# Graph layer and attention layer on one core: projections from block products in float32 to three float32r passes, with another order of layer 0

## The chip, the cores and the metric

The kernel runs on one core of a Trainium2 chip. The metric is the device time of one execution in microseconds (us), the median of several. The profile is of one more execution, taken by the hardware profiler; its durations belong to that execution.

## The reference, cut to what matters

```python
x, adj: (64, 256, 512) float32, (256, 256) int32 (0 or 1)
# layer 0
mi, mj = x @ Wi.T, x @ Wj.T                       # 512 -> 512 each
out = deg[None, :, None] * (mi + b) + einsum('ij,bjo->bio', a, mj)
x = layernorm(x + out)
# layer 1: 8 heads of 64
q, k, v = (x @ W.T + bias for q, k, v)            # 512 -> 512 each
p = softmax(where(adj == 0, -inf, q k^T / 8))
out = (p v, heads side by side) @ Wo.T + bo
x = layernorm(x + out)
```

64 batches of 256 nodes and 512 channels pass through both layers. All is float32.

## The kernel before, in words

A host-side launch (L1085 on) transposes the weights. The device program has a fast path, `unshifted_path` (L237), and a `general_path` (L58) that a flag calls when the fast path's numbers would not hold; it does not run here.

**Tiles.** 128 partitions, so a batch has two row blocks (NT = 2) and four channel blocks (NC = 4). Two batches form a pair (NB = 2), 32 pairs. The main loop (`for g in range(NG - 1)`, L973) runs 31 times: in turn g it makes the attention of pair g, layer 0 of pair g+1, the output projection of pair g, and the query, key and value projections of pair g+1. The opening ahead of it makes layer 0 and the projections of the first pair, and prepares weights; the tail makes the last pair's attention. `in_order` (L281) makes an instruction keep its place in the program's order; all of TensorE's have it, and so the order of the calls in the loop is the order of TensorE's work. Waits come from a framework that sets a semaphore wait wherever an instruction needs a result or a free buffer. Each engine runs its own queue in order.

**Projections.** Each of the four projections of a pair, a 512 x 512 by 512 x 512 product, is done by seven block products of 256 x 256 x 256 (`pair_steps`, L656; Strassen's scheme in Winograd's form), in float32. `left_steps` (L476) makes four sums of blocks of the left side (tiles hS and oS) on VectorE. The weights' sums are made once in the opening (`make_factors`, L411) and kept in DRAM; `bring` (L437) fetches one factor of 256 KB into a ring of nine, in the order of use, by SP's queue. The `use` functions (L680 to L755) evict each product, with adds on VectorE, copies on ScalarE and adds on GpSimd; several products share an intermediate `u`.

**Layer 0.** `l0_steps` (L502) makes one batch's layer 0 from seven products too, but with weights that lie in SBUF (`w0`): step1 to step7, two float32 matmuls of 512 columns each. They use PSUM banks x, y, z, w; x, y and z take two products each, and the second accumulates onto the first after the first has been read: y by step4 then step6, z by step5 then step7. Step5 copies z to `mj`, step6 makes u3 and adds it to `mj` on GpSimd, step7 makes the other half of `mj`. `split` cuts `mj` into a head and a remainder in float32r (`hi` by ScalarE, `lo` by GpSimd), and `neighbours` (L569) multiplies both by the graph's matrix, eight float32r matmuls of 512 columns (tile pa). `take` adds and starts the layer norm, `give` ends it on ScalarE (L466, L467), `send_h` (L598) writes h to DRAM and reads it back in another layout (hB), and `turn_h` transposes blocks on VectorE into hT.

**Attention.** `scores` (L788) makes a pair of heads, adds the mask on VectorE (L809), takes the exponential on ScalarE (L813) and sums two halves on GpSimd (pk, L816). `values` (L837) multiplies by v. `divide` (L876) sums the denominators by a product with ones (den), takes the reciprocal on VectorE (L886), adds it to a total on GpSimd (L887), and copies it by eight DMAs (L894) to the rows where `multiply` (L848) uses it.

**Order in a turn.** `layer0` (L900) cuts the layer-0 steps of the two new batches into slots between the heads' work; in each batch the products follow each other as step4, step5, step6, step7. The second batch's `neighbours` stands after the first output product. Then come the rest of the output projection, query and key, value, with `finish_steps` and `add_output_bias` between them.

Of the kernel before, what the change touches and what calls it, by code (L numbers as in the profile page):

```python
# [16 lines left out]
P = 128  # L17
# [207 lines left out]
def unshifted_path(ctx, tc, flag, x, adj, wiT, wjT, b0, wqT, bq, wkT, bk, wvT, bv, woT, bo, out):  # L225
# [27 lines left out]
    AHEAD = 8  # L253
# [6 lines left out]
    p4 = ctx.enter_context(tc.tile_pool(name="p4", bufs=4))  # L260
    p6 = ctx.enter_context(tc.tile_pool(name="p6", bufs=6))
    stream = ctx.enter_context(tc.tile_pool(name="stream", bufs=AHEAD + 1))
# [35 lines left out]
    def load_x(b):  # L298
        if b < B:
            xh[b] = p6.tile([P, NT, D], F32, tag="xh", name="xh")  # L300
            nc.sync.dma_start(out=xh[b], in_=x[b].rearrange("(t p) d -> p t d", p=P))

    b_bc = p4.tile([P, D], F32, tag="u", name="b_bc")
    xB, hB = {}, {}

    def load_xB(b):
        if b < B:
            xB[b] = p1.tile([P, N // R, P], F32, tag="xB", name="xB")
            for q in range(D // P):
                nc.sync.dma_start(out=xB[b][q * R:(q + 1) * R],  # L310
                                  in_=x[b][:, q * P:(q + 1) * P].rearrange("(r a) n -> r a n", r=R))

# [11 lines left out]
    xT, xS, hT, hS, qT, kT, vv, aoT, oS = ({} for _ in range(9))  # L324


    ident = const.tile([P, P], F32, name="ident")
# [6 lines left out]
    rtot = const.tile([P, N], F32, name="rtot")  # L334
    nc.gpsimd.memset(rtot, 0.0)
# [7 lines left out]
    aT = p3.tile([P, NT, N], F32, tag="pk", name="aT")  # L343
    deg = small.tile([P, NT], F32, tag="deg", name="deg")
# [16 lines left out]
    def check_graph():  # L361


        exact = p1.tile([P, NT, N], F32, tag="oS", name="exact")
# [12 lines left out]
    def load_bias(b, name):  # L377
        t = const.tile([P, NC], F32, tag=name, name=name)
        nc.sync.dma_start(out=t, in_=b)
        d = const.tile([P, 2], F32, tag=name + "d", name=name + "d")  # L380
        return t, d

    bq_sb, bqd = load_bias(bq, "bq")
    bk_sb, bkd = load_bias(bk, "bk")

    def bias_steps():
        for t, d in ((bq_sb, bqd), (bk_sb, bkd)):
            in_order(nc.vector.tensor_sub(d, t[:, 2:4], t[:, 0:2]))

    bv_t = small.tile([P, NC], F32, tag="bvt", name="bv_t")  # L390
    with nc.allow_non_contiguous_dma(reason="512 numbers, once"):
        nc.sync.dma_start(out=bv_t, in_=bv.rearrange("r (c p) -> p (r c)", p=P))
# [3 lines left out]
    def blocks_of(w):  # L396
        return (w.rearrange("(h c p) (j o) -> p h c j o", h=2, p=P, j=2) if w is woT else
                w.rearrange("(p h c) (j o) -> p h c j o", h=2, p=P, j=2))

    sources = {}  # L400
# [717 lines left out]
```

## Time and profile before

| what | us |
|---|---|
| median of 3 runs (3068.2 to 3070.93) | 3068.69 |
| the profiled execution | 3068.79 |
| its span, first to last instruction | 3066.9 |
| one pair in the middle (from store to store) | 94.4 |
| the opening, to 171 us: TensorE busy | 151.3 |
| VectorE TENSOR_TENSOR of 512, mean | 0.69 |
| ScalarE ACTIVATE xh (L467), mean | 0.81 |
| GpSimd TENSOR_TENSOR pk (L816), mean | 1.28 |
| DMA factor from wq, 256 KB, median to landing | 4.2 |
| DMA hB, 512 KB, median to landing | 3.5 |

How to read the profile: the first part of the page has the busy time of each engine and its share of the span, PE being TensorE's matmuls, PEld its weight loads, DVE VectorE, ACT ScalarE, POOL GpSimd. The second part shows the busy share in 40 slices, in tenths. A row of a group has the line, engine, operation, tiles written and read, shapes and count, then after a bar the busy time, the mean in ns, and the idle time of the engine just before, with what ended it. A stretch of the timeline has start and length in us. Successive matmuls overlap, so their cost is the distance from start to start, not the length.

### The profile page before, as it was taken

What the parts mean: (1) busy time and instruction counts of PE and PEld (TensorE: products, weight loads), DVE (VectorE), ACT (ScalarE), POOL (GpSimd) and SP (SyncE); (2) the same over time, 40 slices, a digit from 0 to 9 for tenths busy, and PEclk for the clock granted to TensorE, in tenths of its full rate; (3) what the DMA queues carried; (4) which work ended last, traced back from release to release, by engine and by line L of the source; (5) the groups of instructions that cost most, each with busy time, mean ns of one, the idle gap of its engine ahead of it and who ended that gap; (6) DMA issues with size and microseconds to landing.
All of it is one profiled execution on the core that took longest, in us unless ns stands there. A gap on an engine that the chain in (4) does not pass through costs nothing. (4 is left out here: it accounts for less than half of the span.)

```text
span 3066.9 us, 46810 instructions
## 1 busy us (share of the span) xinstructions
PE 3036.6 (99%) x16646; PEld 2124.6 (69%) x16646; DVE 2178.3 (71%) x3298; ACT 974.1 (32%) x1861; POOL 1519.5 (50%) x1255
## 2 busy tenths in 40 slices
PE   7999999999999999999999999999999999999998
PEld 4667766677766777666776667776677766677665
DVE  6776677766777667777677777677766777767775
ACT  2323333323333333332233332333333333323332
POOL 2544545544545445464454554454544546445453
PEclk9999999999999999999999999999999999999999
DMA  7455544455444555345553445544455444555333
GB/s 255 123 151 159 169 121 136 132 161 166 144 125 127 159 170 155 116 133 154 161 168 119 126 145 160 167 134 134 127 158 170 151 121 128 159 161 166 120 111 96
DMA packets 410411, 447.54 MB, mean 146 GB/s; under 512 B 40896, under 2 KB 300224, under 8 KB 409792
## 3 DMA queue, kind: packets, MB, share of 16 engines
q1 hardware_dynamic: 410176, 444.50, 48.8%
q8 instruction: 136, 2.23, 0.3%
q14 instruction: 99, 0.81, 0.1%
HBM read 340.79 MB, written 70.25 MB: 134 GB/s over the span
## 5 line engine op out<-in xcount | busy, mean ns | idle before, releaser
L461 POOL TENSOR_TENSOR rstd<-ve,mhalf 128x1 f32<-128x1 f32 x256 | 140.5, 552 | 707.3 <-DVE below L459 707.3
L816 POOL TENSOR_TENSOR pk<-pe 128x512 f32<-128x512 f32 x256 | 323.1, 1278 | 322.2 <-ACT pe L813 322.2
L290 PE MATMUL po<-w,xS 128*128 128x512 f32 x1024 | 462.2, 599 | 0.7 <-DVE xS L478 0.7
L290 PE MATMUL st<-hS,factor 128*128 128x256 f32 x2048 | 453.2, 379 | 1.5 <-DVE u L689 1.2
L290 PEld LDWEIGHTS st<-hS,factor 128*128 128x128 f32 x2048 | 388.4, 190 | 56.3 <-DVE xh L744 1.7
L813 ACT ACTIVATE pe<-pe 128x1024 f32<-128x1024 f32 x256 | 270.8, 1058 | 364.4 <-DVE pe L809 364.4
L290 PE MATMUL po<-w,xT 128*128 128x512 f32 x768 | 352.1, 601 | 14.8 <-DVE xS L477 9.3
L290 PE MATMUL st<-hT,factor 128*128 128x256 f32 x1536 | 352.5, 379 | 0.7 <-ACT hT L626 0.7
L290 PEld LDWEIGHTS po<-w,xS 128*128 128x128 f32 x1024 | 189.6, 190 | 235.6 <-issue 206.3
L809 DVE TENSOR_TENSOR pe<-ps,maskT 128x1024 f32<-128x1024 f32 x256 | 298.0, 1195 | 35.4 <-PE ps L290 35.4
L290 PEld LDWEIGHTS st<-hT,factor 128*128 128x128 f32 x1536 | 291.9, 190 | 41.8 <-ACT hT L626 0.9
L886 DVE RECIPROCAL rden<-den 128x256 f32<-128x256 f32 x127 | 222.5, 1752 | 76.6 <-PE den L290 73.6
L290 PEld LDWEIGHTS po<-w,xT 128*128 128x128 f32 x768 | 144.2, 191 | 181.9 <-issue 162.8
L887 POOL TENSOR_TENSOR rtot<-rtot,rden 128x256 f32<-128x256 f32 x127 | 106.8, 841 | 320.1 <-DVE rden L886 320.1
L290 PE MATMUL ps<-qT,kT 64*128 64x256 f32 x2048 | 265.0, 393 | 0.0
L290 PE MATMUL pav<-pe,v_sb 128*32 128x256 f32 x4096 | 248.4, 382 | 1.9 <-ACT pe L813 1.9
L290 PEld LDWEIGHTS ps<-qT,kT 64*128 64x128 f32 x2048 | 184.5, 186 | 78.1 <-issue 38.6
L744 DVE TENSOR_TENSOR xh<-st,xh 128x512 f32<-128x512 f32 x186 | 144.5, 777 | 132.2 <-PE st L290 132.2
L290 PE MATMUL st<-factor,hS 128*128 128x256 f32 x1024 | 234.8, 382 | 0.0
L290 PEld LDWEIGHTS pav<-pe,v_sb 128*32 128x32 f32 x4096 | 119.8, 110 | 164.3 <-issue 95.4
L290 PE MATMUL st<-factor,oS 128*128 128x256 f32 x992 | 224.2, 379 | 0.0
L290 PEld LDWEIGHTS st<-factor,hS 128*128 128x128 f32 x1024 | 192.1, 190 | 35.2 <-issue 10.6
(115 smaller groups left out, 4648.2 us busy)
## 6 DMA issues: line engine op xcount, KB each, us to landing
xB<-in_x_dram SPq DMA_DIRECT2D x256, 128.0 KB, 3.9
xh<-in_x_dram SPq DMA_DIRECT2D x64, 512.0 KB, 4.2
factor<-wq SPq DMA_DIRECT2D x128, 256.0 KB, 4.2
factor<-wk SPq DMA_DIRECT2D x128, 256.0 KB, 2.8
factor<-wv SPq DMA_DIRECT2D x128, 256.0 KB, 2.6
spread<-rden SPq DMA_DIRECT2D x1016, 32.0 KB, 1.9
factor<-wo SPq DMA_DIRECT2D x124, 256.0 KB, 3.2
h_cols<-xh SPq DMA_DIRECT2D x124, 256.0 KB, 3.0
```

Source lines behind the costliest of these rows:

```text
L290: in_order(nc.tensor.matmul(*args, **kw))
L461: nc.gpsimd.tensor_tensor(rstd, ve, mhalf, ALU.pow)
L744: nc.vector.tensor_add(dst, src, dst)
L809: nc.vector.tensor_add(pe.rearrange("p j t q -> p j (t q)"), ps.rearrange("p j t q -> p j (t q)"), maskT.rearrange("p t q -> p (t q)").uns ...
L813: in_order(nc.scalar.activation(flat, flat, AF.Exp, scale=QSCALE, accum_out=etot[:, NB * g + i, pr:pr + 1]))
L816: nc.gpsimd.tensor_tensor(pk, pe[:, :, 0, :], pe[:, :, 1, :], ALU.add)
L886: nc.vector.reciprocal(rden, den)
L887: nc.gpsimd.tensor_tensor(rtot, rtot, rden, ALU.add)
```

## The change

1. The four projections are plain 512 x 512 by 512 x 512 products, each in three passes of float32r. Both sides are cut into a head and a low part that float32r holds, and a third operand is their difference, scaled (Karatsuba): X gets head x head and low x lifted low, Y gets difference x difference, and the output is UP * X + Y. The left side's parts are made by ScalarE (head), VectorE (difference) and GpSimd or VectorE (low). The weights' three parts are made in the first use (`make`), kept in DRAM, and fetched as one tile of 768 KB, in a ring of six.

```diff
+    def make(f, name, j):
+        head, lift, diff = (f[:, i, :].rearrange("p (c o) -> p c o", c=NC) for i in range(3))
+        low = p3.tile([P, NC, P], F32, tag="lu", name="low")
+        for cs, raw in pieces(name, j):
+            in_order(nc.scalar.activation(head[:, cs], raw, AF.Identity, scale=DOWN))
+            in_order(nc.vector.tensor_sub(low[:, cs], raw, head[:, cs].bitcast(F32)))
+            in_order(nc.scalar.activation(lift[:, cs], low[:, cs], AF.Identity, scale=LIFT))
+        in_order(nc.vector.scalar_tensor_tensor(diff, low, LIFT, head.bitcast(F32), ALU.mult, ALU.subtract))
+        nc.sync.dma_start(out=kept[name][j], in_=f.bitcast(F32))
+    def rows_of_product(banks, parts, t, f, c):
+        matmul(X, head, f[:, 0, :], start=first, stop=False, skip_group_check=True)
+        matmul(Y, diff, f[:, 2, :], start=first, stop=end, skip_group_check=True)
+        matmul(X, low, f[:, 1, :], start=False, stop=end, skip_group_check=True)
+    def qk_step(g, store, tag, bias, m, kind):
+            cols_product(banks, hP[g], coming.pop(0))
+            bring()
+            dst = store[g][:, m, :]
+            in_order(nc.scalar.activation(dst, X, AF.Identity, bias=bias[:, m:m + 1], scale=UP))
+            in_order(nc.vector.tensor_add(dst, Y, dst))
```

2. In layer 0, step6 stands before step5, and both halves of `mj` are one VectorE add each; the low part of one half is VectorE's (`lows`).

```diff
-            k["mj"] = p1.tile([P, NT, D], F32, tag="mj", name="mj")
-            nc.vector.tensor_copy(k["mj"][:, 1, :], banks["z"])
 ...
+            in_order(nc.vector.tensor_add(k["mj"][:, 1, :], banks["z"], k["u3"]))
-        return [step1, step2, step3, step4, step5, step6, step7, neighbours, lambda: take(1), lambda: take(0),
-                lambda: give(1), lambda: send_h(b, 1), lambda: give(0), lambda: send_h(b, 0)]
+        return ([step1, step2, step3, step4, step6, step5, step7], neighbours, add, stat, give,
+                lambda: lows(0, nc.vector))
```

3. The turn is written out by hand. Step1 to step3 of the next turn's first batch stand before the output projection, step4 before the last key product; the second batch's neighbour product stands before the last two heads' values.

```diff
+        values(g, 4)
+        values(g, 5)
+        multiply()
+        h11 = turn_h(b1, 1)
...
+        divide_two(g, 5)
+        later = next_scores(6)
+        later(False)
...
+        run(q[5:6])
+        add_pairs(g, 7)
...
+        run(q[6:7])
...
+            next_p[0][0]()
...
+        nb2()
+        add2(1)
+        add2(0)
+        values(g, 6)
+        values(g, 7)
```

4. The heads' channels are arranged so that the reciprocals are copied by four DMAs of 64 KB in place of eight of 32 KB, two of them issued by ScalarE at the last heads; the total of reciprocals is summed by ScalarE.

```diff
+        for half in range(2):
+            for pp in range(2):
+                issuer = nc.scalar if last and pp else nc.sync
+                in_order(issuer.dma_start(out=spread[half * DH:(half + 1) * DH, pp, :],
+                                          in_=rden[pp * DH:(pp + 1) * DH, :]))
+        total(rden, total_out)
```

5. h is read back as two DMAs of 256 KB (one a row block) and transposed in two parts. Most instructions of VectorE, ScalarE and GpSimd, and DMAs, now keep the program's order. Buffers are smaller or shared to make room (xh from six to five, pk from three to two, rden and spread from two to one).

## The prediction

> **What bounds the kernel now.** I read the page's first two parts, then two stretches that halve one pair of batches, then TensorE's instructions in order of time, then single rows.
>
> ```profile
> PE 3036.6 (99%) x16646; PEld 2124.6 (69%) x16646; DVE 2178.3 (71%) x3298; ACT 974.1 (32%) x1861; POOL 1519.5 (50%) x1255
> ...
> PE   7999999999999999999999999999999999999998
> ...
> PEclk9999999999999999999999999999999999999999
> ```
>
> TensorE is busy throughout at full clock, so any matmul time removed is gained and any wait of TensorE is lost in full. The busy time of one pair by stretch (columns: PE, PEld, DVE, ACT, POOL, clock, DMA share, GB/s):
>
> ```profile
> 1044.50:1089.50 45.00, 45.00 (x294) 24.70 (x293) 35.75 (x46) 15.06 (x28) 28.64 (x24) 1.00 0.21 62
> 1089.50:1138.90 49.40, 49.40 (x230) 41.71 (x229) 31.61 (x57) 15.27 (x31) 18.89 (x16) 1.00 0.74 222
> 1044.50:1138.90 94.40, 94.40 (x522) 66.41 (x521) 67.36 (x102) 30.33 (x58) 47.53 (x39) 1.00 0.49 145
> ```
>
> A pair takes 94.4 us, the distance between two stores of results. In its first half (layer 0 and attention) VectorE is busy 35.75 of 45.0 us: little room. In its second half (projections) it has 18 us to spare. TensorE in order of time (start, length, count):
>
> ```profile
> 1003.01 5.34 PE L290 MATMUL st<-factor,oS 128*128 128x256 f32 x24
> 1008.19 1.89 PE L290 MATMUL st<-factor,hT 128*128 128x256 f32 x8
> ```
> ```profile
> 1063.34 0.40 PE L290 MATMUL pa<-lo,graph 128*128 128x512 f32 x1
> 1063.58 0.40 PE L290 MATMUL pa<-hi,graph 128*128 128x512 f32 x1
> 1063.81 0.39 PE L290 MATMUL pa<-lo,graph 128*128 128x512 f32 x1
> ...
> 1064.51 0.40 PE L290 MATMUL pa<-hi,graph 128*128 128x512 f32 x1
> 1064.75 0.39 PE L290 MATMUL pa<-lo,graph 128*128 128x512 f32 x1
> ```
>
> A float32 matmul leaves two records. The 24 records of 256 columns take 5.18 us from start to start, 0.216 each. The neighbour products are the only float32r matmuls here: one record of 512 columns, and (1064.75-1063.34)/6 = 0.235 us from start to start. The rows of three VectorE instructions used below (the last columns: us in all, ns of one, idle before), which overlap by 0.08 us when they follow each other freely:
>
> ```profile
> L809 DVE TENSOR_TENSOR pe<-ps,maskT 128x1024 f32<-128x1024 f32 x256 | 298.0, 1195 | 35.4 <-PE ps L290 35.4
> L886 DVE RECIPROCAL rden<-den 128x256 f32<-128x256 f32 x127 | 222.5, 1752 | 76.6 <-PE den L290 73.6 <-DMA spread<-rden 3.1
> ...
> L563 DVE TENSOR_TENSOR mj<-po,u 128x512 f32<-128x512 f32 x64 | 44.3, 691 | 36.2 <-PE po L290 33.2
> ```
>
> Last, what a wait of TensorE on VectorE costs, once, in the opening:
>
> ```profile
> 80.84 3.72 PE L290 MATMUL st<-hS,factor 128*128 128x256 f32 x16 [1.23 <-DVE u L689]
> ```
>
> [...] 512 float32 columns take two records of 0.429 us, 0.858 in all, against 0.235 for float32r, 3.65 times. [...] here a 0.74 share moves 222, so 300 at full share with rows of 1 and 2 KB.
>
> **Part 1, the projections.** Before: four projections of seven block products, four float32 matmuls each, two records: 224 records x 0.216 = 48.4 us a pair. After: four of 16 matmuls in three passes: 192 x 0.235 = 45.1. Saved: 3.3 us a pair on the path. Bounds: at 0.216 it is 6.9, at 0.238 (the slowest starts among the neighbour products) 2.7. I take 0.235: same shapes, same kind of operands, 64 groups alike.
>
> **Part 2, VectorE, ScalarE and GpSimd.** A pair loses on VectorE the block sums hS and oS (8 x 0.69), the output adds L744 (5 x 0.69 + 1.2), the qkv adds (10 x 0.69 + 4 x 0.48) and two copies L548: about 20 us. It gains 8 + 4 adds and 4 x (0.74 + 0.69) for outputs, seven differences (4 + 2 of 512, one of 1024) and two low parts that were GpSimd's: about 22. The sum hardly moves, but of the new work the low parts, the attention output's differences and a quarter of the h transposes stand in the first half. ScalarE goes from 30 to about 37 us, GpSimd from 47 to about 41 (the sums of inverses, `mj` and output adds go, low parts come). Both are covered by 90 us of TensorE. One new wait stands on ScalarE: the sum of inverses there waits for the reciprocal, and the two steps of a norm and an exponential stand behind it; the exponential's mask add follows that reciprocal on VectorE anyway, so only the norm loses up to 2 us, which is in the h block's way below.
>
> **Part 3, the order of layer 0 (the decisive part).** Before, the products alternate z, y, z, so 1.72 us of matmuls hide each eviction. After, y's two halves stand together (step4, step6) and z's (step5, step7), and the second half accumulates onto a bank that VectorE must have read first. In the built program three such pairs stand next to each other on TensorE in every pair of batches, with nothing between: z of the first batch, y and z of the second. Three waits result that the kernel before doesn't have.
> A, z of the first: last record's tail 0.17, 0.04 to start, the add 0.69 (the L563 row's length), 0.06 back, a restart 0.1: 1.05 us. The 1.23 above bounds it from over, 0.95 from under.
> B, y of the second: between step2's end and this eviction VectorE has queued: scaled add 0.66, four sums of x 2.3, two adds 1.2, two statistics groups 2.1, reciprocal 1.68, two mask adds 2.25, scaled add 0.66, the eviction 0.69 = 11.5, with 0.3 of hand-over. TensorE meanwhile has neighbours 2.06, values 1.75, den 0.55, scores 2.0, two products 3.43 = 9.8. It waits 2.0 (1.0 with VectorE on time; 2.9 if the sums take their slow form).
> C, z of the second: from step6's start TensorE reaches step7 after 7.8 us (step6, values, den, scores, step5). VectorE evicts u3, waits for the returned h block, transposes 1.1, then reciprocal 1.68, mask adds 2.25, eviction 0.69. The store to h_cols and the read back take 3.0 and somewhat under 3.5 us by the DMA list, behind a GpSimd power and two ScalarE steps, so the block is there about 4.5 us after step6's start, and step7 starts at about 10.1: 2.3 lost (1.0 to 3.4). Behind these waiting instructions stand all attention matmuls.
> D, the factors: 16 of 768 KB a pair in place of 28 of 256 KB. The third and fourth of wv are issued only after wo's are consumed, behind a store and two reads of h on SP's queue, whose second read waits about 3 us for the store. 1024 KB landed in 5.4 to 13.4 us, 256 KB in 2.6 to 4.9; I take 4.5, which leaves 0.6 of waiting (0 to 2). Later ones have one step of slack or more.
> Stalls: 1.05 + 2.0 + 2.3 + 0.6 = 5.95. Against 3.3 saved: +2.65 us a pair.
>
> **Part 4, the rest.** Layer 0 ahead by one more product moves work between pairs, not its sum; the second neighbour product needs step7, so it inherits C. Four inverse copies for eight take four issues of 0.59 us off SP at each of 127 places; SP isn't on the path, and it costs or gains nothing, except that it frees the queue ahead of h, contained in C. The opening has 171.0 - 151.3 = 19.7 us of idle TensorE already; 12 factors made there at about 1.6 us of VectorE each, with nothing else to run on TensorE for the first four, add an estimated 10 us (0 to 20).
>
> **Sum.** 31 pairs x 2.65 = 82, + 10: +92 us. The profiled execution took 3068.8 us (span 3066.9), as the median, 3068.7. Forecast 3161 us.
>
> **Rivals.** The pitch (0.24): in long float32r runs TensorE keeps 0.216, a tail of switching in short groups being the reason for 0.235. Place: the 45 us of projections. Saved 6.9 - 5.95 = 0.95 a pair, -29 + 10: 3050 us, faster; it decides below 0.219. [...] against: 0.231 to 0.238 right to a group's end. With VectorE on time as well it gives 2963.
> VectorE on time (0.12): all three round trips bare, 3.15, no D: 3.3 saved, nearly nothing left, + 10: 3074 us. For it: 18 us of VectorE room in the second half; against: in-order queues fix what stands ahead of the evictions in the first half.
> DMA short (0.06): 12.6 MB of factors and some 3.5 of the rest in the second half at 300 GB/s need 54 us for 46 of TensorE; even a third of that left over gives about 3240. Against: larger rows, and six of the loads fall into the first half.
> That the change doesn't do what it says: the float32r passes stand in the built program, so this is excluded.
>
> **Numbers.** Forecast 0.58, own range 3110 to 3225. Below 3000 I leave 0.1 (part of the pitch), above 3225 0.07. Faster by over 0.2% (about what a measurement of this kernel can tell from no change): 0.24 and a little of VectorE on time, 0.27; within 0.2%: 0.07; slower: 0.66.
>
> **What would show it.** In the trace after: projections 0.235 from start to start (right) or 0.216; waits of PE `po` on VectorE `mj` and `u`, three a pair of 1 to 2.5 us; PE busy under 97%. If these waits are missing or under 0.8 us each, part 3 is wrong; if PE waits on `factor` DMAs for more, D is.

## The result and the profile after

The changed kernel takes 3305.64 us (median of 4 runs, 3303.63 to 3307.09), the kernel before 3069.32 in the same comparison: ratio 1.0769, 95% interval 1.075 to 1.0788. It is slower by 236 us; forecast were 92.

The page of the changed kernel, busy time by engine, then two rows of the slices:

```profile
PE 3002.5 (91%) x15638; PEld 1920.6 (58%) x15638; DVE 2287.3 (69%) x3413; ACT 1208.5 (37%) x2247; POOL 1442.8 (44%) x1056
...
PE   6898999999999999999999999999999898999998
...
PEclk8999999999999999999999999999999999999999
```

TensorE is busy 34 us less than before and idle 9% of the span. One pair of the changed kernel in two stretches (attention and layer 0; projections), columns as before:

```profile
2253.90:2309.70 55.80, 50.70 (x309) 26.07 (x309) 42.41 (x50) 21.58 (x41) 26.46 (x19) 0.97 0.38 125
2309.70:2354.60 44.90, 42.38 (x182) 33.48 (x180) 28.67 (x56) 15.55 (x28) 19.16 (x15) 1.00 0.72 263
sum 100.70, PE 93.08 PEld 59.54 DVE 71.08 ACT 37.13 POOL 45.61; mean PE 46.54 PEld 29.77 DVE 35.54 ACT 18.56 POOL 22.81
```

A pair takes 100.7 us here, before 94.4. The first stretch has 5 us in which TensorE waits, and a granted clock of 0.97. Who TensorE waited for (sum in us, times, longest):

```profile
PE po L290 <- DVE u L555: 78.3, 31, 2.6
PE po L290 <- DVE mj L564: 64.0, 63, 2.3
PE px L290 <- DMA factor<-wv: 41.1, 43, 2.0
PE pa L290 <- DVE lo L538: 27.7, 30, 0.9
PE pxy L290 <- DMA factor<-wq: 23.8, 19, 2.0
```

The `u` line is round trip B of the prediction, 2.5 us in each of 31 turns. The `mj` line holds A and C; taken apart by their place in the pair they are 0.78 and 1.26 on average (C from 0.90 to 2.28). The other three are the factors (D) and a wait that I had not foreseen, for the low part ahead of the second neighbour product. Some waits of a projection are put down by the trace to VectorE (`pxy` on `kT`, `st` or `below`, 0.6 us a pair in all); I count them with the factors, since they are gone in e2, which moves only a load.

What a wait costs beyond its own length is seen behind B, TensorE in order of time:

```profile
2286.81 2.50 PE L290 MATMUL po<-w,xS 128*128 128x512 f32 x4 [2.49 <-DVE u L555]
2289.23 3.05 PE L290 MATMUL pav<-pe,v_sb 128*32 128x256 f32 x32
2292.11 0.60 PE L290 MATMUL den<-pk,ones 128*32 128x256 f32 x8
```

and three stretches of 3.4 us at that place (the column after POOL is the granted clock):

```profile
2284.70:2288.10 3.40, 1.29 (x3) 0.68 (x4) 3.40 (x4) 3.24 (x7) 1.32 (x2) 1.00 0.65 161
2288.10:2291.50 3.40, 3.40 (x26) 1.10 (x28) 1.68 (x3) 0.00 (x0) 2.46 (x2) 0.51 0.50 140
2291.50:2294.90 3.40, 3.40 (x41) 2.19 (x34) 2.92 (x3) 1.37 (x3) 1.27 (x1) 0.99 0.78 217
```

The value products take 3.05 us and not 1.93, since the clock is halved for the 3.4 us after the wait. In the loop the granted clock, as the trace records it, changes only at the edges of windows of 3.41 us, and stands at half for one or two of them at a time. In this execution 41 such windows are at half clock (half-clock windows below), in the one before 3, none of them in the loop.

Where the 236 us are: the first value product starts at 137.7 us, before at 103.6, so 34 us are lost in the opening; the 31 turns take 3124.9 us, before 2920.5, which is 204 us; the tail is alike. From the third to the 30th turn a pair is 6.5 us longer: TensorE's idle time is 8.2 (A, B, C together 4.6; factors 2.7; low part 0.9; before 0.01), half-clock windows cost 1.4 (78.5 us of them in 28 pairs, counted as half lost), and what remains, its work at full clock, is 3.1 less.

### The profile page after: what moved, and what is told of

It reads as the page before. It is cut to its first block, busy times and chain, and to the rows that moved or that the text cites. A ratio compares the mean times of both kernels' runs of the same rounds, so it can differ in the third digit from the quotient of the medians.

```text
span 3305.3 us, 42785 instructions
## 1 busy us (share of the span) xinstructions
PE 3002.5 (91%) x15638; PEld 1920.6 (58%) x15638; DVE 2287.3 (69%) x3413; ACT 1208.5 (37%) x2247; POOL 1442.8 (44%) x1056
## 2 busy tenths in 40 slices
DMA packets 305606, 609.50 MB, mean 184 GB/s; under 512 B 27632, under 2 KB 189424, under 8 KB 305136
## 5 line engine op out<-in xcount | busy, mean ns | idle before, releaser
L290 PE MATMUL po<-w,xS 128*128 128x512 f32 x1024 | 517.2, 634 | 142.7 <-DVE u L555 78.3
L616 POOL TENSOR_TENSOR hL<-hF,hA 128x512 fp32r<-128x512 f32 x124 | 206.6, 1666 | 219.7 <-ACT hA L610 219.7
L701 DVE TENSOR_TENSOR kT<-py,kT 128x512 f32<-128x512 f32 x128 | 88.6, 692 | 275.1 <-ACT kT L700 275.1
L610 ACT ACTIVATE hA<-hF 128x512 fp32r<-128x512 f32 x124 | 78.3, 632 | 386.5 <-DVE hF L496 386.5
L478 ACT ACTIVATE xh<-xh,shift,rstd 128x512 f32<-128x512 f32 x256 | 208.8, 815 | 8.5
L373 POOL TENSOR_TENSOR xh<-xh,degb 128x1024 f32<-128x1024 f32 x64 | 153.4, 2397 | 130.3 <-DMA xh<-in_x_dram 101.3
L616 POOL TENSOR_TENSOR v<-aoT,qT 128x512 fp32r<-128x512 f32 (+1 forms) x93 | 167.5, 1816 | 76.2 <-PE pav L290 53.2
L290 PE MATMUL px<-hA,factor 128*128 128x512 f32 x640 | 185.1, 411 | 0.0
L825 POOL TENSOR_TENSOR aoT<-aoT,spread 128x512 f32<-128x512 f32 x127 | 182.0, 1433 | 3.4 <-DMA spread<-rden 3.3
L290 PE MATMUL py<-hD,factor 128*128 128x512 f32 x640 | 176.3, 397 | 5.1 <-ACT kT L700 5.1
```

The costliest lines, as they stand in the source:

```text
L290: in_order(nc.tensor.matmul(*args, **kw))
L373: in_order(nc.gpsimd.tensor_tensor(xh[b], xh[b], degb, ALU.add))
L478: order(nc.scalar.activation(t, t, AF.Identity, bias=shift, scale=rstd))
L610: in_order(nc.scalar.activation(parts[0], src, AF.Identity, scale=DOWN))
L616: in_order(engine.tensor_tensor(parts[1], src, parts[0].bitcast(F32), ALU.subtract))
L701: in_order(nc.vector.tensor_add(dst, Y, dst))
```

## Experiments

Times are medians; ratios are to the kernel before in the same comparison. The changed kernel (3306 us, 1.077) is the base unless another is named.

**e1: the order alone, in the kernel before** (with the sum that goes with it: one VectorE add for a copy and a GpSimd add).

```diff
-        return [step1, step2, step3, step4, step5, step6, step7, neighbours, ...
+        inner = [step6, step5] if adjacent else [step5, step6]
+        return [step1, step2, step3, step4, *inner, step7, neighbours, ...
...
-                nc.vector.tensor_copy(k["mj"][:, 1, :], banks["z"])          # step5
+                nc.vector.tensor_add(k["mj"][:, 1, :], banks["z"], k["u3"])
```

> The kernel before, with only the order of layer 0 taken from the change (in the loop, second halves of y and of z directly behind the first ones). Theory A (each adjacency costs TensorE a round trip through VectorE): three waits of TensorE `po` on `u` and `mj` a pair, 0.8 to 1.0 us where VectorE has nothing queued, up to 2.5 where it has; 2.7 to 4.2 us a pair over 31 pairs on 3069 us: 3153 to 3199 us. Rival (VectorE's queue, not the adjacency, made the waits in the changed kernel; the kernel before has the room): waits under 0.4 us each, below 3105 us.

Measured: 3176.69 us, 1.0354 (1.0337 to 1.0372). TensorE's waits in it:

```profile
PE po L290 <- DVE mj L549: 58.1, 62, 1.1
PE po L290 <- DVE u L543: 26.1, 31, 0.8
```

There are three bare round trips, waits of 0.8, 0.8 and 1.1 us: 2.7 us of idle time a pair (76.0 us in 28 pairs), and 0.8 more in the records around them (`po<-w,xS` is busy 426.5 us in 28 pairs against 404.1): 0.27 a trip, so 1.17 us a trip. No half-clock window is added in the loop: no wait there exceeds 1.1 us. Theory A holds: in the kernel before, the order alone costs 108 us.

**e2: the load of x taken out of the way of a factor.**

```diff
         turn_x(b3 + 1)
-        load_xB(b3 + 2)
-        run([v[3], v[2], end[0], ...
+        run([v[3], v[2]])
+        load_xB(b3 + 2)
+        run([end[0], ...
```

> The changed kernel, with the load of the next-but-one batch's x (four transfers on SP's queue that wait for a VectorE transpose) moved behind the last of v's products, so that the second wq factor isn't queued behind it. Theory H (the wait of 1.4 us a pair for wq is SP's queue standing still behind that load): it goes, 3306 - 31 x 1.4 = 3262 us. Rival D (the factor transfers are short of DMA rate): the wait stays or moves to the next factor, 3295 to 3315 us.

Measured: 3245.53 us, 1.0582 (1.0565 to 1.06). SP's queue in the changed kernel, and then in e2 (start, length of issue):

```profile
2332.70 2.58 SPq L310 DMA_DIRECT2D xB<-in_x_dram  x4
2335.38 0.54 SPq L441 DMA_DIRECT2D factor<-wq  x1
```
```profile
2282.32 0.32 SPq L441 DMA_DIRECT2D factor<-wq  x1
...
2284.75 2.75 SPq L310 DMA_DIRECT2D xB<-in_x_dram  x4
```

The second wq factor could have been asked for when v's last product let its slot go, but SP stood at four loads of x, which waited for a transpose on VectorE and took 2.6 us to issue. In e2 the wait for wq is gone. The gain is 60 us, not 43: half-clock windows fall from 41 to 32, which is an estimated 15 us more. Theory H holds, and Rival D (short of DMA rate) falls. The wait for wv stays:

```profile
PE px L290 <- DMA factor<-wv: 40.6, 41, 2.2
```

**e3: steps 3 and 4 of the second batch exchanged.**

```diff
-        run(q[2:4])
+        run([q[3], q[2]])
```

> The changed kernel, with steps 3 and 4 of the second batch exchanged, so that step 3's four matmuls (1.72 us) stand between the first and the second half of y and VectorE takes u2 ahead of step 3's scaled add. Theory C (a wait of over about 1.95 us inside one of the throttle's windows of 3.41 us costs a half-clock window after it as well): the wait of 2.5 us shrinks to under 0.4 and some 22 half-clock windows go with it, 3306 - 31 x 2.2 - 22 x 1.7 = 3200 us, half-clock windows down from 41 to under 20. Rival (half-clock windows have nothing to do with that wait): 3306 - 68 = 3238 us with some 40 such windows still there. Rival (VectorE bounds the first half, so the wait only moves on): above 3275 us.

Measured: 3313.45 us, 1.0788 (1.077 to 1.0806): nothing is gained; the last rival holds, the wait moves on. My working was wrong in one point: step 3's matmuls stood ahead of step 6 in either order, so TensorE comes to step 6 no later; only VectorE's queue is shorter, by one scaled add of 0.66. B falls from 2.53 to 1.87, and C grows from 1.26 to 2.62, with 42 half-clock windows. VectorE in e3, between the sum of y and step 7's:

```profile
2184.52 0.72 DVE L559 TENSOR_TENSOR u<-po,u 128x512 f32<-128x512 f32 x1
2186.80 1.14 DVE L496 STREAM_TRANSPOSE hF<-hB 128x512 f32<-128x512 f32 x1 [1.56 <-DMA hB<-h_cols]
```

VectorE waits for the h block's read, and the reciprocal, the mask adds and step 7's sum stand behind it. B's delay had hidden that.

**e4: the products of layer 0 alternating again.**

```diff
-        return ([step1, step2, step3, step4, step6, step5, step7],
+        return ([step1, step2, step3, step4, step5, step6, step7],
...
+            in_order(nc.gpsimd.tensor_tensor(k["mj"][:, 1, :], k["mj"][:, 1, :], k["u3"], ALU.add))   # step6
...
-            in_order(nc.vector.tensor_add(k["mj"][:, 1, :], banks["z"], k["u3"]))
+            in_order(nc.vector.tensor_copy(k["mj"][:, 1, :], banks["z"]))                              # step5
```

> The changed kernel with the products of layer 0 alternating between the two banks again (steps 4, 5, 6, 7; the first half of z copied out by VectorE, u3 added to it on GpSimd), all else as changed. Theory A: the three waits on `u` and `mj` (4.6 us a pair) and most half-clock windows (1.3 us a pair) go, 3306 - 31 x 5.9 = 3123 us. Rival G (the added GpSimd step makes the lower row's rounding late, so that the neighbour product waits 1 to 2 us): 3155 to 3185 us. Rival V (VectorE bounds the first half whatever the order): above 3240 us.

Measured: 3388.87 us, 1.1058 (1.1029 to 1.1087), 83 us slower than with the waits: Rival V, with G's mechanism in it. A, B and C are gone, but TensorE in e4 has a new first wait, and VectorE shows from where:

```profile
PE pa L290 <- ACT hi L534: 76.3, 31, 5.0
```
```profile
2338.31 1.13 DVE L496 STREAM_TRANSPOSE hF<-hB 128x512 f32<-128x512 f32 x1 [3.21 <-DMA hB<-h_cols]
```

TensorE runs ahead, VectorE stands 3.2 us at the h block, then u3, the added GpSimd step and the rounding are late, and the neighbour product waits 2.5 us (mean). TensorE's idle time is alike in both orders, 8.8 and 8.2 us a pair. So in the changed kernel the adjacency is not what bounds this stretch: VectorE's queue is, with the h block in it. Of the 2.7 us by which a pair of e4 is longer, some 1.6 are half-clock windows (170.7 us of them in 28 pairs against 78.5).

**e5: the sums of x earlier.**

```diff
-        run(q[0:2])
-        sum_x(b2)
+        sum_x(b2)
+        run(q[0:2])
```

> The changed kernel, with the four sums of the second batch's x moved ahead of the scaled add of its step 2 on VectorE, into 1.6 us in which VectorE has nothing to do there. Theory Q (VectorE's in-order queue from those sums to the sums of y sets when step 6 may start, 11.3 us without a gap against 9.8 us of TensorE): the wait on `u` falls from 2.5 to about 0.9 us, all behind it (norm, h block, step 7) comes 1.6 us earlier, 3306 - 31 x 1.6 = 3256; and as no wait exceeds 1.95 us in a throttle window, the 23 half-clock windows of the loop go too, 1.7 us each: 3217 us with under 20 such windows in the run. Rival (the wait moves to step 7, as when steps 3 and 4 were exchanged): above 3285 us. Rival (half-clock windows don't follow that wait): 3256 us with some 40 windows.

Measured: 3314.74 us, 1.0797 (1.0779 to 1.0815); B is 2.65, so neither the theory nor the first rival's mechanism is right. The four sums in e5:

```profile
2175.66 0.41 DVE L488 TENSOR_TENSOR xS<-xT 128x256 f32<-128x256 f32 x1
2176.11 1.38 DVE L489 TENSOR_TENSOR xS<-xS,xT 128x256 f32<-128x256 f32 x1
2177.41 1.52 DVE L490 TENSOR_TENSOR xS<-xT 128x256 f32<-128x256 f32 x1
2178.85 1.50 DVE L491 TENSOR_TENSOR xS<-xT,xS 128x256 f32<-128x256 f32 x1
```

The idle time that I moved them into was that in which GpSimd makes two pair sums (`pk`, 2.8 us there) and a product (1.46), and beside these a sum takes 1.4 to 1.5 us. Alone a sum takes 0.41 to 0.42. In the changed kernel one of the four was slow (2.7 us for all): it takes 1.40 us (from 2276.08) beside such a product (1.47, from 2275.71), and the next two, with GpSimd idle, take 0.41. Here three are slow (4.7). Why the two engines slow each other isn't shown.

**e9: the same sums where GpSimd has nothing to do** (ahead of the reciprocal behind step 7 of the first batch).

```diff
         run(p[4:7])
+        sum_x(b2)
...
         run(q[0:2])
-        sum_x(b2)
```

> The changed kernel, with the same four sums moved once more, now ahead of the reciprocal and the mask adds behind step 7 of the first batch, where GpSimd has nothing to do for 5 us. Theory P (a 256-column sum on VectorE takes 0.41 us alone and 1.4 to 1.5 beside a GpSimd operation on SBUF; that ate the gain of the last move, 4.7 us for the four): they take 1.7 us here, VectorE reaches u2 2.7 us earlier against the changed kernel, the wait on `u` falls from 2.5 to 0.9 or less, and no wait exceeds 1.95 us in a window: 3306 - 31 x 1.6 - 23 x 1.7 = 3217 us, under 20 half-clock windows. Rival M (the exponentials are 1.6 us later, and the value products 2 and 3 wait for them instead): 3255 to 3300 us.

Measured: 3235.96 us, 1.0542 (1.0524 to 1.0559). The sums in e9:

```profile
2216.60 0.42 DVE L488 TENSOR_TENSOR xS<-xT 128x256 f32<-128x256 f32 x1
2217.06 0.42 DVE L489 TENSOR_TENSOR xS<-xS,xT 128x256 f32<-128x256 f32 x1
2217.40 0.42 DVE L490 TENSOR_TENSOR xS<-xT 128x256 f32<-128x256 f32 x1
2217.73 0.42 DVE L491 TENSOR_TENSOR xS<-xT,xS 128x256 f32<-128x256 f32 x1
```

They take 1.5 us in place of 2.7 in the changed kernel and 4.7 in e5, and what stood behind them comes earlier:

```profile
PE po L290 <- DVE u L555: 29.2, 31, 0.9
```

B is 0.94, as Theory P has it, and half-clock windows fall from 41 to 22; the exponentials don't come too late (Rival M). In the loop a pair is 2.1 us shorter: 1.1 of idle time, and 1.0 of half clock (23.9 us of it in 28 pairs in place of 78.5). C grows to 1.90, by the h block, which takes 20 us of the gain; so the time stays 19 us over what Theory P has.

**e8: one wait a pair put into the kernel before.**

```diff
+    def hold():
+        d = bank("hold")
+        matmul(d[:, :P], ones, ones, start=True, stop=True)
+        in_order(nc.vector.tensor_copy(held, d[:, :P]))
+        for _ in range(4 - 1):
+            in_order(nc.vector.tensor_reduce(held[:, :1], ...
+        matmul(d[:, :P], ones, held, start=True, stop=True)
+        ...
...
-        return [p[:3] + [item(turn_x, b2)] + p[3:4],
+        return [p[:1] + [hold] + p[1:3] + [item(turn_x, b2)] + p[3:4],
```

> The kernel before, with one added wait of TensorE in each of the 31 passes of the loop: between step 1 and step 2 a 128-column product of ones, then four VectorE operations one after the other that end in its copy, then a 128-column product of that copy; nothing else uses them. The wait is about 0.2 + 0.3 + 3 x 0.69 + 0.15 = 2.7 us, the products 0.3. Theory C (a wait of over 1.95 us in one throttle window of 3.41 us brings a half-clock window): 31 x 3.0 = 93, and 65% of the waits lie in one window far enough, 20 x 1.7 = 34 more: 3195 us, some 20 half-clock windows. Rival (the half-clock windows of the changed kernel come from its float32r projections, not from waits): 3161 us, 3 half-clock windows as before.

Measured: 3209.82 us, 1.0462 (1.0444 to 1.0479). The wait:

```profile
PE hold L290 <- DVE held L937: 78.9, 31, 2.5
```

The waits are 2.54 us each, and there are 24 half-clock windows in place of 3, with no float32r projection in the kernel: Theory C holds. The edges of the half-clock windows lie on one grid of 3.4133 us, so the idle time in every window can be summed. In the loop, each of the 23 windows after one with 2.07 to 2.55 us of this wait in it is at half clock, and none after one with up to 1.98. Turns without such a window take 97.7 to 98.2 us, turns with one 99.1 to 99.6: 1.5 us a window.

**e17 and e18: where the h block is late.** e17 is e9 with ScalarE's order changed (the sum of inverses of `divide_two(g, 3)` kept back), e18 is e17 with the stores of h ahead of the copies of inverses on SP's queue (ScalarE's copy of the values, 0.6 us, moves behind the norms with them; in e17 the norms already end as early in the turn as in e18):

```diff
-        later = next_scores(4)       # e17
         give1(0)
         send_h(b1, 0)
+        later = next_scores(4)
         later()
+        sums_left.pop()()
```

```diff
-        divide_two(g, 3)             # e18
         give1(1)
         send_h(b1, 1)
         give1(0)
-        send_h(b1, 0)
+        send_h(b1, 0, False)
+        divide_two(g, 3)
+        read_h(b1)
         later = next_scores(4)
```

> e9_sums_alone, and in addition, on ScalarE, the sum of the second pair of inverses (which waits there for the reciprocal, with both rows' norms behind it) moved behind the exponentials 4 and 5, and the second norm ahead of exponential 4. Theory N (this wait holds the norms of the first batch back by some 2 us, so its h block comes late, and VectorE, which waits 2.1 us for it in its queue, reaches the second batch's step 7 late): the h block is there when VectorE comes to it, the second batch's wait on `mj` falls from 1.9 to about 0.9, 3236 - 31 x 1.0 - 6 x 1.7 = 3195 us. Rival (VectorE's own work fills that stretch): the wait stays at 1.5 or more, 3220 us or more.

> e17_norm_early, and in addition the two stores of the first batch's h block put on SP's queue ahead of the four copies of inverses, and its two reads behind them (ahead of the stores these copies stand 2.4 us of issues after the reciprocal they wait for). Theory S (SP's queue held the stores, so that the norms' 2 us in e17 were lost there): the block lands some 2.5 us earlier, VectorE doesn't wait for it, the second batch's wait on `mj` falls from 1.9 to about 0.8: 3243 - 31 x 1.1 - 10 = 3199 us. Rival (VectorE's own work fills that stretch): the wait stays at 1.5 or more, 3225 us or more.

Measured: e17 3243.23 us, 1.0564 (1.0546 to 1.0582), C still 1.88; e18 3207.78, 1.0455 (1.043 to 1.0479), C 0.91. SP's queue in e17, then in e18, then VectorE at the h block in e18:

```profile
2228.89 12.10 SPq L882 DMA_DIRECT2D spread<-rden  x8
2241.04 1.16 SPq L632 DMA_DIRECT2D h_cols<-xh  x2
```
```profile
2207.78 1.40 SPq L632 DMA_DIRECT2D h_cols<-xh  x2
2209.41 2.39 SPq L885 DMA_DIRECT2D spread<-rden  x4
```
```profile
2215.28 1.19 DVE L496 STREAM_TRANSPOSE hF<-hB 128x512 f32<-128x512 f32 x1 [0.19 <-DMA hB<-h_cols]
```

Theory N falls by itself: in e17 the two norms end 2.7 and 3.7 us earlier in the turn than in e9 (the second at 2238.5 here), and the stores are issued where they were (here at 2241.0), since four copies of inverses stand ahead of them, each issue some 0.6 us, waiting for the reciprocal. With the stores ahead the block lands 1.9 us earlier (median), it is there when VectorE comes to it (0.19 us), and C is a bare round trip. Theory S holds.

**e10: v's products in halves** (on e2: the first two factors for both rows of the first batch, then the third and fourth).

```diff
-        run([o[2], v[1]])
-        sum_x(b3)
-        v[0]()
+        o[2]()
+        v_two(g + 1, "SMSA")
+        sum_x(b3)
...
+        for cs in ((0, 1), (2, 3)):          # in v_two
+            for t in (1, 0):
+                for c in cs:
+                    rows_of_product(banks[t], hP[g], t, coming[c], c)
```

> The changed kernel with the load of x behind v's products (3246 us as measured) and, in addition, the first two v products taken in two halves each (the first two factors for both, then the third and fourth for both), so that the third wv factor is needed six matmuls (1.36 us) later. Theory R (the wait of 1.3 us a pair for wv is a slot of the ring given free too late for a landing of 5.4 us): it falls to 0.2, 3246 - 31 x 1.1 = 3212 us. Rival D (the rate of the factor transfers): the wait moves to wv's fourth factor or to wq, above 3235 us.

Measured: 3200.94 us, 1.0426 (1.0409 to 1.0444). The wait for wv falls from 40.6 us in all to 12.0, the time by 45 us against e2:

```profile
PE px L290 <- DMA factor<-wv: 12.0, 17, 2.0
```

Theory R holds: wo's last factors hold their slots of the ring until the last output product, and a landing of 5.7 us (median) doesn't fit into the two products until wv's third is needed.

**e6, e7: too much moved.** e6 is e5 with e3's exchange and the first batch's h transpose behind `low2()`; e7 is e6 with both steps 7 behind other products, the last value products ahead of the second neighbour product, and e2.

```diff
-        h11 = turn_h(b1, 1)          # e6
-        split_head(*h11)
-        split_low(*h11, nc.gpsimd)
         divide_two(g, 5)
...
-        split_diff(*h11)
         low2()
+        h11 = turn_h(b1, 1)
+        split_head(*h11)
+        split_low(*h11, nc.gpsimd)
...
         add2(0)
+        split_diff(*h11)
```
```diff
-        run(p[4:7])                  # e7
+        run(p[4:6])
...
         values(g, 1)
+        run(p[6:7])
         divide_two(g, 1)
...
-        run(q[6:7])
...
             next_p[0][0]()
+        run(q[6:7])
...
+        values(g, 6)
+        values(g, 7)
         nb2()
```

> As the last one, and in addition steps 3 and 4 exchanged (which alone brought nothing) and the transpose of the first batch's h block moved on VectorE from between u3 and the reciprocal to behind the low part of step 7. Theory Q: exchanging steps 3 and 4 brought nothing only since VectorE then waited for the h block ahead of step 7's sum; with that gone, the wait on `u` falls to about 0.2 and the second batch's on `mj` stays bare at 0.9: 3217 - 31 x 0.7 = 3195 us. Rival (VectorE's work itself, not its wait for h, fills the stretch up to step 7): no better than 3217 us, the second batch's `mj` wait over 1.5 us.

> The last one, and in addition: step 7 of the first batch behind the first two value products, step 7 of the second batch behind the next pair's step 1, the second neighbour product behind the last two value products, and the load of x behind v's products. Theory: round trips A and C (0.8 and 0.9), the low part's wait (0.9) and wq's (1.4 to 2) are covered as well, 3195 - 31 x 4.2 = 3065 us, about the time of the kernel before, with only wv's wait of 1.3 a pair left. Rival V (VectorE's or ScalarE's queue is late by then and TensorE waits at the exponentials or at the projections of o instead): 3110 to 3170 us.

Measured: 3412.94 us, 1.113 (1.1107 to 1.1154), and 3364.05, 1.0963 (1.0945 to 1.0981), both far over what I expected (e6's rival had no upper end, but its sign, an `mj` wait over 1.5 us, is not there). In e6 C is bare (0.90), but B still 1.99 (the sums take their slow form), and the h transpose stands now where VectorE and GpSimd make the output projection's inputs: waits for a bank that the last reciprocal frees (1.2 us a pair), for GpSimd's low part (0.6), for ScalarE's head (0.5) and more for wv (1.9) come anew. So the transpose's place in VectorE's queue costs on either side: early it waits for the block, late it holds back what stands behind it.

**e11 to e15: one after the other.** e11 is e9 and e2 with e3's exchange and e7's first move, and:

```diff
         values(g, 5)
+        run(q[5:6])
         multiply()
...
-        run(q[5:6])
         add_pairs(g, 7)
-        split_diff([head[:, :, :N], None, diff[:, :, :N]], aoT[g][:, :, :N])
         run(q[6:7])
-        split_diff(*h11)
         low2()
+        split_diff([head[:, :, :N], None, diff[:, :, :N]], aoT[g][:, :, :N])
+        split_diff(*h11)
```

e12 adds e10's halves. e13, and then e14 (in `qk_step`, and alike in `v_step`):

```diff
-        split_head([head[:, :, :N]], aoT[g][:, :, :N])
         add_pairs(g, 7)
         run(q[6:7])
         low2()
+        split_head([head[:, :, :N]], aoT[g][:, :, :N])
...
+        values(g, 6)
+        values(g, 7)
         nb2()
```
```diff
             cols_product(banks, hP[g], coming.pop(0))
-            bring()
...
             in_order(nc.vector.tensor_add(dst, Y, dst))
+            bring()
```

e15 on VectorE:

```diff
-        split_diff(*h11)
...
-        split_diff(*ao_parts(g, 1, upper))
...
-        add2(1)
-        add2(0)
...
         divide_two(g, 7)
+        add2(1)
+        add2(0)
+        split_diff(*ao_parts(g, 1, upper))
+        split_diff(*h11)
```

> The changed kernel with the sums ahead of the reciprocal, the load of x behind v's products, step 7 of the first batch behind the first two value products, steps 3 and 4 of the second exchanged, its step 5 in front of the scores 6 and 7 (so that these stand between the halves of z), and the low part of its step 7 ahead of two differences on VectorE. Theory: 3217 (as above) less 60 for wq, and 31 x (0.8 + 0.7 + 0.9 + 0.5) = 90 for round trips and the low part: 3067 us. Rival V (VectorE's queue takes over: waits of TensorE on the exponentials or the value and score banks): 3110 to 3170 us.

> The last one, and in addition the first two v products in two halves. Theory R: 31 x 1.1 = 34 us less than the last one, about 3033 us, faster than the kernel before. Rival D: within 10 us of the last one.

> e12_apart_v_split, and in addition, around the second neighbour product: the head of the attention output (1.04 us on ScalarE) behind the rounding of step 7's sum and not ahead of it, and the last two value products (1.75 us) ahead of the neighbour product. Theory W (the pair has no other stall left than the 2.8 us a pair in which the neighbour product waits for ScalarE's rounding and the low part, and what half-clock windows these bring): they fall to about 0.5, 31 x 2.3 = 71 us less, and some 15 of the 34 half-clock windows with 1.7 us each go: 3141 - 71 - 25 = 3045 us, faster than the kernel before (3069). Rival V (the stall moves to the output projection's inputs on GpSimd and VectorE, or to the score banks, as in e7_combined): 3100 us or more.

> The last one, with the making or bringing of the next factor written behind the evictions of a projection step and not ahead of them. In the opening, where a factor is made by ScalarE and VectorE in some 2 us, the evictions stood behind that and TensorE waited for the banks (up to 3.8 us); in the loop only SP's DMA moves. Theory O (part of the opening's 34 us is this order): the waits on ScalarE's `kT` (5.1 us) and some of the half-clock windows after them go, 8 to 14 us less than the last one. Rival (the making itself, 16 factors one after the other, sets the opening): within 3 us of the last one.

> e14_evict_first, and in addition, behind the second neighbour product, the last reciprocal and the two adds of the neighbour sums ahead of two differences (for the upper half of the second batch's attention output, and for the h block) on VectorE; these took 2.8 and 1.8 us beside two GpSimd low parts, where such a one takes 0.7 alone. Theory P (VectorE's SBUF-only operations beside GpSimd made the reciprocal late, and through it the output projection waits 3 us a pair for its bank, its heads, differences and low parts): 3186 - 31 x 2.5 - 15 = 3093 us, a pair at the 94.4 us of the kernel before, the rest being the opening. Rival (the loop has another bound): 3150 us or more.

| kernel | us | ratio (95%) | a pair, us | half-clock windows |
|---|---|---|---|---|
| e11 | 3174.78 | 1.0349 (1.0332 to 1.0366) | 96.8 | 25 |
| e12 | 3140.91 | 1.0229 (1.0212 to 1.0246) | 95.8 | 34 |
| e13 | 3188.49 | 1.0394 (1.038 to 1.0408) | 97.1 | 24 |
| e14 | 3186.44 | 1.0384 (1.037 to 1.0398) | 97.1 | 26 |
| e15 | 3108.28 | 1.0121 (1.0104 to 1.0138) | 94.6 | 14 |

e11 and e12 were both 108 us over what I expected (e12's step from e11, 34 us, came as Theory R has it): with A, B, C covered (other products stand between the halves), the wait went on to the second neighbour product (TensorE in e12):

```profile
2279.94 0.73 PE L290 MATMUL pa<-hi,graph 128*128 128x512 f32 x2 [1.85 <-ACT hi L574]
...
2281.74 1.22 PE L290 MATMUL pa<-lo,graph 128*128 128x512 f32 x2 [0.51 <-DVE lo L538]
```

e13 covered that, and lost 48 us (its Rival V): three differences on VectorE now ran beside GpSimd's low parts, and the reciprocal stood behind them (VectorE in e13):

```profile
2306.65 2.31 DVE L613 SCALAR_TENSOR_TENSOR kT<-qT,aoT 128x1024 fp32r<-128x1024 f32 x1
2308.88 2.83 DVE L613 SCALAR_TENSOR_TENSOR hD<-hA,hF 128x512 fp32r<-128x512 f32 x1
2311.64 1.76 DVE L613 SCALAR_TENSOR_TENSOR kT<-qT,aoT 128x512 fp32r<-128x512 f32 x1
```

The middle one takes 2.83 us, and 0.69 at other places of e13; the last takes 1.76, and 0.69 in the changed kernel with GpSimd idle. With the reciprocal ahead of two of them (e15) 78 us come back, 15 less than Theory P has. Most turns of e15 then take 94.0 to 94.8 us, as those of the kernel before; its TensorE still waits 2.3 us a pair. By the profiled executions e15 is 42 us over the kernel before (spans 3108.6 and 3066.9): 27 in the opening and 15 in the 31 turns, 5.5 of these in the last. No version that I ran beats the kernel before.

**e16: the opening.**

```diff
             in_order(nc.scalar.activation(head[:, cs], raw, AF.Identity, scale=DOWN))
-            in_order(nc.vector.tensor_sub(low[:, cs], raw, head[:, cs].bitcast(F32)))
-            in_order(nc.scalar.activation(lift[:, cs], low[:, cs], AF.Identity, scale=LIFT))
-        in_order(nc.vector.scalar_tensor_tensor(diff, low, LIFT, head.bitcast(F32), ALU.mult, ALU.subtract))
+            in_order(nc.vector.tensor_copy(lift[:, cs], raw))
+            in_order(nc.vector.tensor_copy(diff[:, cs], raw))
```

> The changed kernel, with the making of a factor in the opening cut to three independent copies of the raw weight (one on ScalarE, two on VectorE): the low part, its lift and the difference are left out, so the factors don't hold the split weights. Theory S (a factor made by ScalarE, VectorE, ScalarE in turn, 1.9 us each, 16 of them, sets the opening): the first value product comes at 115 to 122 us in place of 138, and the time is 16 to 23 us less, 3283 to 3290. Rival (the loads, the order of evictions or the waits for the first batches set it): first value product above 130 us, time within 7 us of 3306.

Measured: 3282.62 us, 1.071 (1.0675 to 1.0746); the first value product starts at 119.8 us, the changed kernel's at 137.7. It leaves out the low part, its lift and the difference. Theory S of that run holds for 18 of the 34 us: TensorE is idle 8.7 us less up to there, and at half clock for 17 us less, which costs about half of that. One factor of the changed kernel (ScalarE):

```profile
56.99 0.61 ACT L448 ACTIVATE factor<-raw 128x512 fp32r<-128x512 f32 x1
58.36 0.63 ACT L450 ACTIVATE factor<-low 128x512 fp32r<-128x512 f32 x1 [0.76 <-DVE low L449]
58.90 0.61 ACT L448 ACTIVATE factor<-raw 128x512 fp32r<-128x512 f32 x1
```

It is 1.91 us from one head to the next: ScalarE stands 0.76 us for VectorE's low part, with the next head behind it. e16 takes away this waiting and the work together, so it doesn't tell them apart. e14's exchange brought 3 us in the opening, within the rival's range.

## Why the prediction was wrong in size, step by step

Right were the direction, the work saved, and that the three round trips through VectorE's in-order queue wait. The step that failed is the sum of stalls in part 3, "1.05 + 2.0 + 2.3 + 0.6 = 5.95": it measured 8.2. D, put at 0.6, was 2.7, and the low part, put at nothing, 0.9. With it failed the first sentence on TensorE, "any wait of TensorE is lost in full": a wait that puts some 2 us into one window of 3.41 us (from 1.96 on in the changed kernel, with one exception, and from 2.07 on in e8) is followed by a window at half clock, 1.4 us a pair that the sum has at nothing. In the opening, 10 us were 34. "The decisive part" was too much said of the order: it costs 108 us in the kernel before (e1), but to take it back in the changed kernel makes it slower still (e4, 83 us).

| a pair, us | predicted | measured | |
|---|---|---|---|
| TensorE's work at full clock | -3.3 | -3.1 | part 1 |
| A | 1.05 | 0.78 | part 3 |
| B | 2.0 | 2.53 | part 3 |
| C | 2.3 | 1.26 | part 3 |
| D, wv and wq | 0.6 | 2.7 | part 3 |
| low part before the second neighbour product | 0 | 0.9 | not foreseen |
| half-clock windows | 0 | 1.4 | not foreseen |
| sum | 2.65 | 6.5 | |

- **Part 1** held. The median from start to start in the projections is 0.227 us, 192 of them 43.6; with the first records after a change of tile (0.63 us to the next start where the projections begin) and the half-clock windows the projections are busy 45.9 us a pair (45.1 predicted). The rival of a 0.216 pitch is out: measured before was 0.216 for float32 records of 256 columns, and no trace showed it for float32r.
- **Part 2**: VectorE (71.1 us a pair) and ScalarE (37.1) came about as worked out; GpSimd was 45.6 and not 41. Wrong was the use of durations taken alone: beside GpSimd a VectorE operation with both inputs in SBUF takes up to four times as long (a sum 1.52 in e5 against 0.42 in e9, a difference 2.83 against 0.69 in e13), and GpSimd's take longer too (1.75 against 1.27 in e13). I had named a slow form of the sums, and priced it into B's upper bound only.
- **Part 3, A to C**: 4.57 us together against 5.35. B and C are one chain: what shortens B lengthens C (e3, e9) as long as the h block is late. That the block is late was right; the place was not the norm but SP's queue, where four copies of inverses stand ahead of its stores (e17, e18). Part 4 had counted what four copies fewer free there, and otherwise said "SP isn't on the path"; the four that remain hold the stores until the reciprocal.
- **Part 3, D**: "Later ones have one step of slack or more" was the largest miss. The second wq factor stood behind the load of x on SP's queue (e2, 60 us), and wv's third and fourth behind slots freed too late (e10, 45 us). I had looked at the queue at wv's place alone, and there taken 4.5 us for a landing that has a median of 5.7. By the prediction's own sign (more waits on `factor`) it is D that was wrong. The rate wasn't short: the changed kernel moves 263 GB/s at a share of 0.72 in its second stretch, an estimated 365 at full share, where the prediction's 222 at 0.74 gave 300; over the whole execution its mean packet is 1.99 KB (609.50 MB in 305606), and 1.09 before (447.54 in 410411).
- **The low part** of step 7 is needed by the last two of the eight neighbour matmuls; I counted C for it and not the rounding and the subtraction behind C, of which the subtraction takes 1.76 us there, beside GpSimd. No run takes this wait away by itself.
- **Clock**: the loop of the kernel before has hardly a wait, so its trace couldn't show it. e8 measures it by itself, e9 in the changed kernel.
- **Part 4**: 34 us in place of 10. TensorE is idle 15.4 us longer there, and at half clock for 30.7 us in place of 3.4, which loses 13.7; some 5 are work in another place. Half of it is the making of the factors (e16): 16 are made there and not 12, and my 1.6 us of VectorE a factor left out that ScalarE and VectorE wait for each other (1.9 us a factor).

Of the 144 us missing in the forecast, 24 are the opening and some 120 the turns: per pair D 2.1, half clock 1.4, low part 0.9, the work 0.2, less 0.8 for A to C. What stays open is the rest of the opening, and whether e15 with e18's order and a shorter opening would come below the kernel before; it wasn't tried.

## What to carry to other kernels

A wait of TensorE is priced with what it triggers: here those that put 2.07 us or more into one window of 3.41 us cost a further 1.5 us (e8). Follow each queue's order (SP's too) from the instruction that is late back to the one that stands ahead of it, since a wait that is covered turns up at the next in-order queue: of three moves against B, e3 and e5 gained nothing and e9 70 us. Take a VectorE duration from a place where GpSimd does what it will do there, not from the row's mean.

## What the runs showed of the hardware that I had not expected

- The clock falls to half for one window of 3.41 us after a window with 2.07 us or more of a single wait in it, and not after up to 1.98 (e8). In the changed kernel the border is between 1.95 and 1.96, with one exception at 1.66. Idle time isn't the whole measure: in e13 1.34 to 1.53 us were enough 13 times, and in other windows up to 1.53 were not; the records beside its waits also stand further apart (0.34 us in place of 0.23), which the idle time doesn't count.
- A window that is itself at half clock needs less idle time to be followed by another: in the changed kernel 0.72 and 0.73 us did it, and up to 0.56 did not. In e4 19 of the loop's 57 half-clock windows came so, after 0.35 to 1.33 us.
- A VectorE sum of 256 columns with both inputs in SBUF: 0.42 us alone (e9), 1.4 to 1.5 beside GpSimd (e5); a difference of 512: 0.69 alone (`kT<-qT,aoT`, changed kernel), up to 2.83 beside GpSimd (e13). It isn't each such pair that slows VectorE: in e13 at 2325.36 a difference takes 0.69 beside a low part of GpSimd, which takes 1.81 and not 1.28.
- A round trip TensorE, VectorE, TensorE on one bank: 0.78 (changed kernel) to 1.1 us (e1) of idle time, and 0.27 in the records around it (e1).
